# Two layers on a 128-node graph: scores placed behind attends, banks kept for them, splits and first mixes moved, last division in halves

## The chip, the core and the metric

The kernel runs on one core of one Trainium2 chip. The metric is the device time of one execution in microseconds. Engines are named as in the profile: PE is TensorE, DVE VectorE, ACT ScalarE, POOL GpSimd, SP SyncE, which here issues every DMA.

## The reference

The input is x, 128 batches of 128 nodes with 512 features, and one 128 by 128 adjacency matrix. Two layers follow each other:

```python
# layer 0
h = relu(layernorm(x))
x = x + (einsum('nm,bmd->bnd', adj, h) @ weight + bias)
# layer 1: masked attention, 8 heads of 64
h = relu(layernorm(x))
q, k, v = split(h @ w_qkv)
attn = softmax(where(adj == 0, -inf, q @ k.T * 64**-0.5))
o = (attn @ v) @ w_proj + b_proj
x = x + o + (layernorm(o) * gamma + beta)
```

All is float32. Where precision asks for it, the kernel splits both factors of a product into a high and a low part and adds three products in a faster number format (fp32r) instead of one plain float32 product.

## The kernel before

**Stages.** The first stage (`phase1`) does layer 0 batch by batch. For each batch it makes the statistics, the ReLU, the product with the adjacency matrix ("mix", L483), splits that product in three parts (L430 to L432), multiplies them with the split weight `wA` (L442, twelve matmuls of 512 columns for a batch), and adds (L450, L455). The first `FIRST` = 4 batches use a plain float32 product instead (L492), because the split weight isn't made yet; there a copy of the mix by ACT (L487) stands between mix and product. The results go to DRAM.

The second stage (`phase2_group`) does layer 1 in 32 groups of four batches, each group as two pairs. `fetch` reads a pair back, normalises it, transposes it through DRAM, and splits it in three parts in the tile `hp`, which has room for three pairs. A group computes Q and K for all four batches (L580, 96 matmuls), and V for each batch (L442 on `wv`, 12 each, summed into a `v` tile at L615 and L616). For each pair, `scores_of` computes the scores (L637, in 64-row halves of the PE array), masks them (L645), takes the row maximum (L650), the exponentials (L657), the reciprocal (L661) and the division (L662, POOL), and sends them through DRAM to be transposed. A group later, `rest_of` lets them land, transposes 32 by 32 blocks (L678), multiplies with V ("attend", L696, in 64-column halves of the array), projects, and adds the last normalisation. The projection takes the split weight `wA1` (L442), or, for the last three pairs, the plain one (L714).

A pair's `rank` counts from the end: rank 0 is the last pair, rank 1 the one before it, ranks 3 and 2 the two pairs of the group before. The pair of rank 0 isn't sent through DRAM: PE flips its tiles (L684).

**What sets the order.** Nothing is ordered by hand. Every operation is put into a `Plan` with its engine, an estimated length, the tiles that it reads and writes, and either a due time or, on PE, a wished time (`at`). `schedule` then walks through a model of the core: whenever an engine is free, it takes, of the operations whose inputs are there, the one with the smallest priority whose tiles have a free place. The programs of the engines follow that order. Three details matter here:

- Tiles share places by name. `ps` are the eight PSUM banks `b0` to `b7`; a pair's scores take two banks for each batch, an attend two, each split product two. `f0` to `f3` hold the scores (`s`) and the transposed probabilities (`pT`) of phase 2. `qk` has eight places, so a group's Q and K can only be overwritten when the scores of the group before are done.
- An operation that finds no free place is passed over, and a later one may take the place that it waits for (L139 to L156).
- An operation in split-array mode has the mark `tiled`. The plan counts 0.15 us (`turn`) for a change of mode, and an operation that keeps the mode has its priority improved by 2 (`stay`).

The parameter `early`, where it is given, is the earliest planned time at which an operation may start.

**Lines that matter.** The wait of the landings is the argument `gate` of `rest_of`; it is set at L590 and again at L610:

```python
        if rests:
            rests.pop(0)(gate)
        gate = scores(0)
        ...
        if len(rests) > 1:
            rests.pop(0)(gate)
        scores(1)
```

Of the kernel before, what the change touches and what calls it, by code (L numbers as in the profile page):

```python
# [15 lines left out]
P = 128  # L16
# [40 lines left out]
class Plan:  # L57
# [44 lines left out]
    def schedule(self):  # L102
# [22 lines left out]
        while len(order) < len(self.ops):  # L125
# [6 lines left out]
            for e in self.ENGINES:  # L132
# [5 lines left out]
                stay = p["stay"] if e == "PE" else 0.0  # L138
                for item in sorted(avail[e], key=lambda i: (i[0] - (stay if self.ops[i[1]].tiled == tiled else 0.0), i[1])):  # L139
                    o, taken = self.ops[item[1]], []  # L140
                    for b in o.bufs:
# [10 lines left out]
                    for b in taken:  # L152
                        b.slots.places[b.name], b.name = 0.0, None
                        b.slots.next -= 1
                else:
                    continue  # L156
# [37 lines left out]
    "stretch": 1.5, "margin": 0.4, "crowd": 2.0,  # L194
# [4 lines left out]
def kernel(  # L199
# [36 lines left out]
    def named(prefix, *numbers):  # L236
# [14 lines left out]
        "wA": group(["wA"]), "ident": group(["t8"]), "ident2": group(named("t", 8, 14)), "raw2": group(named("t", 20, 24)),  # L251
# [79 lines left out]
    op("DVE", 1.4, mask_ops, r=[adj_sb], w=[adj_sb, some, maskb], due=30)  # L331


    def split_weights(w, c, col, raw, low, due, gap):
# [3 lines left out]
        op("ACT", 0.63, lambda: nc.scalar.activation(h(), raw.ap, AF.Copy, scale=CUT), r=[raw], w=[(w, (0, part))], due=due)  # L338
        op("DVE", 0.69, lambda: nc.vector.tensor_tensor(low.ap, raw.ap, h().bitcast(F32), op=ALU.subtract),
           r=[raw, (w, (0, part))], w=[low], due=due + gap)  # L340
        op("ACT", 0.62, lambda: nc.scalar.activation(l(), low.ap, AF.Copy, scale=K), r=[low], w=[(w, (1, part))], due=due + 2 * gap)
        op("DVE", 0.69, lambda: nc.vector.scalar_tensor_tensor(s(), low.ap, K, h().bitcast(F32), op0=ALU.mult, op1=ALU.subtract),
           r=[low, (w, (0, part))], w=[(w, (2, part))], due=due + 2 * gap)
# [22 lines left out]
    def stats(srcs, how, place, due=None, plain=False, junk=None, first=None):  # L366
# [8 lines left out]
        if how == "DVE":  # L375
            for n, src in enumerate(srcs):
                def bn(n=n, src=src):
                    nc.vector.bn_stats(t.ap[:, 6 * n:6 * n + 6], src.ap)  # L378
                    nc.vector.bn_aggr(t.ap[:, 12 + 2 * n:14 + 2 * n], t.ap[:, 6 * n:6 * n + 6])
                op("DVE", 0.87, bn, r=[src], w=[(t, n)], due=dues[0], what="bn")  # L380
# [85 lines left out]
    def phase1(batches):  # L466
# [4 lines left out]
        t, arg = stats([X[i] for i in batches], "DVE" if batches[0] < FIRST + 2 else "ACT", "st1", junk=[View(junk, lambda ap: ap)] * 2)  # L471
        for n, i in enumerate(batches):
# [11 lines left out]
            MIX[i] = op("PE", 0.9, mix, r=[h0, adjT], w=[p], at=ti - (1 if i == 0 else 3.75), what="mix")  # L484
# [68 lines left out]
    rests, raw2, final = [], [], []  # L553

    def phase2_group(j):
# [54 lines left out]
        gate = scores(0)  # L610
        for n, i in enumerate(group):
# [3 lines left out]
            op("ACT", 0.6, lambda v=v, a=a: nc.scalar.activation(v.ap, a.ap, AF.Copy, scale=UP), r=[a], w=[v], due=tv + 2.5, what="vA")  # L615
            op("DVE", 0.69, lambda v=v, b=b: nc.vector.tensor_tensor(v.ap, b.ap, v.ap, op=ALU.add), r=[b], w=[v], due=tv + 4, what="vB")  # L616
# [3 lines left out]
        if not left:  # L620
# [3 lines left out]
            op("POOL", 0.6, lambda: make_identity(nc, ident2.ap), w=[ident2], what="ident", after=[b.writers[-1][1]])  # L624

    def scores_of(pair, place, QK, rank, at_scores):

        S = []
        for n, i in enumerate(pair):
# [8 lines left out]
            last = op("PE", 0.85, scores, r=list(QK.values()), w=ps, at=ts, what="scores", tiled=True)  # L638
# [19 lines left out]
            for g in range(4):  # L658
                op("ACT", 1.16, lambda g=g, exps=exps: exps((2 * g, 2 * g + 1)), r=[(mx, "m")], w=[(s, ("e", g)), (mx, g)],
                   due=ts + 6 + 2.3 * g + 9.2 * n if rank else ts + 4 + 1.2 * g + 4 * n, what="exp")  # L660
            op("DVE", 0.18, lambda mx=mx: nc.vector.reciprocal(mx.ap[:, H:], mx.ap[:, H:]), w=[mx], what="rec", due=ts + 15 + 9.2 * n)  # L661
            op("POOL", 1.93, lambda heads=heads, mx=mx: nc.gpsimd.tensor_tensor(  # L662
                heads().rearrange("p h q r -> p q h r"), heads().rearrange("p h q r -> p q h r"),
# [128 lines left out]
```

## Time and profile before

| | us |
|---|---|
| three runs: lowest, median, highest | 2163.84, 2164.19, 2164.22 |
| the profiled execution | 2163.97 |
| its span, first to last instruction | 2162.2 |
| PE busy | 2147.0 |
| DVE busy | 1721.4 |
| POOL busy | 1524.2 |
| ACT busy | 1480.0 |
| mean granted PE clock | 0.999 of full speed |

The span is what the trace shows; the execution's own time has 1.8 us more around it. PE is busy for 99% of the span, but ends of matmuls are modelled, so that a busy PE isn't PE at its peak: the spacing between the starts of matmuls tells more. In rows of a timeline or of the chain of waits, the first number is the start in us from the beginning of the span, the second the length; xN counts the instructions that the row merges; a bracket gives the idle time before the row and what ended it. A float32 matmul appears as two instructions.

### The profile page before, as it was taken

How to read it: one execution, taken by the hardware profiler on the slowest of the kernel's cores; microseconds unless marked ns; L12 is line 12 of the kernel's file. 1: busy time of each engine (PE TensorE's matmuls, PEld its weight loads, DVE VectorE, ACT ScalarE, POOL GpSimd, SP SyncE). 2: the span in 40 equal slices, each digit the busy share in tenths (PEclk: the TensorE clock that was granted, in tenths of full speed). 3: DMA queues.
4: the chain of work that ended last, by engine and by line, in shares of the span. 5: the costliest groups of instructions: out<-in, count | busy, mean ns of one | idle time of the engine just before them, and what ended most of it. 6: DMA issues, size and time to landing. Idle time of an engine off the chain costs nothing.

```text
span 2162.2 us, 40584 instructions
## 1 busy us (share of the span) xinstructions
PE 2147.0 (99%) x12811; PEld 1778.6 (82%) x12811; DVE 1721.4 (80%) x3271; ACT 1480.0 (68%) x4238; POOL 1524.2 (70%) x1276
## 2 busy tenths in 40 slices
PE   9999999999999999999999999999999999999998
PEld 7888888888878888888888888888888888888885
DVE  7998888885877778777777777878777777777777
ACT  7887777767666666666666666666666666666653
POOL 6887878784667666666667777777667777777755
PEclk9999999999999999999999999999999999999999
DMA  7766666665656666666655556566666666556653
GB/s 245 244 217 228 218 217 217 225 225 161 176 166 195 183 188 182 190 185 182 180 176 176 176 176 183 179 185 184 193 184 185 186 180 196 177 180 182 185 176 118
DMA packets 297863, 410.69 MB, mean 190 GB/s; under 512 B 33072, under 2 KB 163248, under 8 KB 297648
## 3 DMA queue, kind: packets, MB, share of 16 engines
q1 hardware_dynamic: 297648, 408.09, 62.0%
q8 instruction: 102, 1.67, 0.3%
q14 instruction: 113, 0.93, 0.1%
HBM read 207.68 MB, written 200.28 MB: 189 GB/s over the span
## 4 chain that ended last, share of the span: by engine, by line
PE 92%; DVE 1%; POOL 0%; DMA 0%; issue 0%; ACT 0%; SPq 0%; POOLq 0%; DVEq 0%; ACTq 0%
PE b L442 44%; PE b L580 32%; PE b L637 6%; PE b L696 5%; PE b L483 4%; DVE t L730 0%; POOL f L662 0%; DMA f<-d 0%; DVE t L728 0%; DMA out_dram<-t 0%; POOL m L384 0%; DVE m L378 0%; DVE t L716 0%; ACT t L539 0%; SPq L267 0%
## 5 line engine op out<-in xcount | busy, mean ns | idle before, releaser
L442 PE MATMUL b<-wA,t 128*128 128x512 f32 x2952 | 750.4, 393 | 2.2 <-DVE t L431 1.2
L580 PE MATMUL b<-hp,wqk 128*128 128x512 f32 x3072 | 738.8, 390 | 0.8 <-ACT t L587 0.8
L580 PEld LDWEIGHTS b<-hp,wqk 128*128 128x128 f32 x3072 | 574.1, 188 | 124.9 <-issue 4.5
L442 PEld LDWEIGHTS b<-wA,t 128*128 128x128 f32 x2952 | 544.7, 188 | 111.3 <-DVE t L431 2.0
L722 POOL TENSOR_TENSOR t<-t,t 128x512 f32<-128x512 f32 x126 | 163.3, 1297 | 419.9 <-DVE t L453 297.5
L657 ACT ACTIVATE f<-f,n 128x128 f32<-128x128 f32 x1024 | 397.0, 391 | 2.1
L442 PE MATMUL b<-wv,hp 128*128 128x512 f32 x1536 | 388.2, 395 | 0.8 <-DVE t L453 0.8
L442 PEld LDWEIGHTS b<-wv,hp 128*128 128x128 f32 x1536 | 283.2, 188 | 65.9 <-DVE t L453 1.2
L587 ACT ACTIVATE t<-b 128x512 f32<-128x512 f32 x256 | 151.7, 593 | 241.6 <-PE b L580 241.4
L645 DVE TENSOR_TENSOR f<-b,maskb 128x512 f32<-128x512 f32 x256 | 166.3, 683 | 138.0 <-PE b L696 74.2
L662 POOL TENSOR_TENSOR f<-f,n 128x1024 f32<-128x1024 f32 x128 | 246.1, 1923 | 31.1 <-DVE n L661 31.1
L430 ACT ACTIVATE t<-b 128x512 fp32r<-128x512 f32 x246 | 145.2, 590 | 106.4 <-PE b L483 83.4
L547 POOL TENSOR_TENSOR hp<-t,hp 128x512 fp32r<-128x512 f32 x128 | 163.5, 1300 | 55.1 <-ACT hp L546 55.1
L588 DVE TENSOR_TENSOR t<-b,t 128x512 f32<-128x512 f32 x256 | 172.8, 676 | 34.8 <-PE b L580 24.3
L657 ACT ACTIVATION_READ_ACCUMULATOR f<-f,n 128x1 f32 x1024 | 194.5, 190 | 0.0
L431 DVE TENSOR_TENSOR t<-b,t 128x512 fp32r<-128x512 f32 x246 | 167.0, 679 | 22.5 <-ACT t L430 22.1
L432 DVE SCALAR_TENSOR_TENSOR t<-t,b 128x512 fp32r<-128x512 f32 x246 | 166.5, 677 | 0.0
L726 POOL TENSOR_TENSOR t<-t,t 128x512 f32<-128x512 f32 x122 | 158.0, 1295 | 9.5
L550 POOL TENSOR_TENSOR hp<-hp 128x512 fp32r<-128x512 f32 x128 | 164.0, 1303 | 0.6
L725 POOL TENSOR_TENSOR t<-t,gamma_b 128x512 f32<-128x512 f32 x122 | 158.0, 1295 | 8.1 <-ACT t L724 8.1
L678 DVE STREAM_TRANSPOSE f<-f 128x1024 f32<-128x1024 f32 x126 | 156.0, 1238 | 5.8 <-DMA f<-d 5.0
L650 DVE TENSOR_REDUCE n<-f 128x8 f32<-128x1024 f32 x128 | 155.1, 1212 | 1.3
(119 smaller groups left out, 3133.5 us busy)
## 6 DMA issues: line engine op xcount, KB each, us to landing
d<-f SPq DMA_DIRECT2D x126, 512.0 KB, 3.3
f<-d SPq DMA_DIRECT2D x504, 128.0 KB, 4.4
t<-x1d SPq DMA_DIRECT2D x128, 256.0 KB, 4.2
d<-t SPq DMA_DIRECT2D x128, 256.0 KB, 3.0
t<-d SPq DMA_DIRECT2D x512, 64.0 KB, 3.7
t<-x1b SPq DMA_DIRECT2D x128, 256.0 KB, 3.8
out_dram<-t SPq DMA_DIRECT2D x128, 256.0 KB, 3.4
t<-in_x_dram SPq DMA_DIRECT2D x91, 256.0 KB, 3.0
```

Source lines behind the costliest of these rows:

```text
L431: op("DVE", 0.69, lambda: nc.vector.tensor_tensor(l.ap, p.ap, h.ap.bitcast(F32), op=ALU.subtract), r=[p, h], w=[l], what=name + "l")
L432: op("DVE", 0.69, lambda: nc.vector.scalar_tensor_tensor(s.ap, h.ap.bitcast(F32), UP, p.ap, op0=ALU.mult, op1=ALU.subtract), r=[p, h], w=[ ...
L442: nc.tensor.matmul(p.ap, lhsT=parts[m][2]()[:, c], rhs=w.ap[:, m, c, :], start=start and c == 0, stop=stop and c == C - 1)
L547: op("POOL", 1.35, lambda ht=ht, h=h, l=l: nc.gpsimd.tensor_tensor(l(), ht(), h().bitcast(F32), op=ALU.subtract), r=[h1, HP[i, 0]], w=[HP[ ...
L550: op("POOL", 1.38, lambda l=l, s=s: nc.gpsimd.tensor_tensor(s(), s().bitcast(F32), l().bitcast(F32), op=ALU.subtract), r=[HP[i, 1]], w=[HP ...
L580: nc.tensor.matmul(p.ap, lhsT=wqk.ap[:, which, c, col:col + P], rhs=hp[:, pick, :, which, c, :], start=start and c == 0, stop=stop and c = ...
L588: op("DVE", 0.69, lambda r=r, b=b: nc.vector.tensor_tensor(r.ap, b.ap, r.ap, op=ALU.add), r=[b], w=[r], due=tg + (4 if g < 7 else 2), what ...
L645: op("DVE", 0.68, lambda e=e, heads=heads, ps=ps: nc.vector.tensor_tensor(heads()[:, e * C:(e + 1) * C], ps[e].ap.rearrange("p c (q r) -> ...
L657: nc.scalar.activation(v[:, h], v[:, h], AF.Exp, bias=mx.ap[:, h:h + 1], scale=scale, accum_out=mx.ap[:, H + h:H + h + 1])
L662: op("POOL", 1.93, lambda heads=heads, mx=mx: nc.gpsimd.tensor_tensor(heads().rearrange("p h q r -> p q h r"), heads().rearrange("p h q r ...
L722: op(eng, us, lambda x1=x1, o=o, unit=unit: unit.tensor_tensor(x1.ap, x1.ap, o.ap, op=ALU.add), r=[o], w=[x1], due=tl + (3 if rank > 1 els ...
L725: op("POOL", 1.32, lambda o=o: nc.gpsimd.tensor_tensor(o.ap, o.ap, gamma_b.ap, op=ALU.mult), r=[gamma_b], w=[o], due=tl + 7, what="gamma")
```

## The change

The edits fall into five groups.

- **Planner.** An operation in split mode that finds no free place now keeps its kind of place: for the rest of that pass, no lower operation that needs a new place of that kind is taken. If the array is already in split mode and enough places come free within 0.6 us (`wait`), PE takes nothing until then.
- **Order in phase 2.** Scores of ranks above 2 must follow the last attend that was put into the plan. The landings of the second pair are gated by the fifth product of Q and K, no longer by the first scores of the group. Block transposes are due 3 us earlier, the two halves of V's sum 1.5 and 2 us.
- **Start.** The mask may not start before 13.5, the statistics of batch 1 not before 6.2, the splits of the first weight not before 12 to 16.5; mixes of batches 0 to 5 are wished 4.9 us ahead of their product, not 3.75. (Batch 0 wished 1 ahead, as before.)
- **Weight splits.** The twelve splits of `w_qkv`, each with its load, go with every third pair of phase 1 from the seventh pair on, not with every pair from the fifth on.
- **End.** Rank 2 projects with the split weight; the exponentials, reciprocal and division of rank 1 have earlier due times; rank 0 takes reciprocal and division in two halves of four heads, each flip waiting for its half; the identity for the flips is made in the tile of the means, near the end of the last group's due times.

```diff
@@ schedule
                 stay = p["stay"] if e == "PE" else 0.0
+                held = []
                 for item in sorted(avail[e], ...):
                     o, taken = self.ops[item[1]], []
+                    if held and any(b.slots in held for b in o.bufs if b.slots and not b.name):
+                        continue
...
                     for b in taken:
                         b.slots.places[b.name], b.name = 0.0, None
                         b.slots.next -= 1
+                    if o.tiled:
+                        held.append(b.slots)
+                        if tiled:
+                            soon = sorted(v for v in (b.slots.places[n] for n in b.slots.names) if v is not None)
+                            want = sum(x.slots is b.slots and not x.name for x in o.bufs)
+                            if len(soon) >= want and soon[want - 1] <= t + p["wait"]:
+                                held = None
+                                break
                 else:
+                    held = None
+                if held is None:
                     continue
...
-    "stretch": 1.5, "margin": 0.4, "crowd": 2.0,
+    "stretch": 1.5, "margin": 0.4, "crowd": 2.0, "wait": 0.6,
@@ start
-    op("DVE", 1.4, mask_ops, r=[adj_sb], w=[adj_sb, some, maskb], due=30)
+    op("DVE", 1.4, mask_ops, r=[adj_sb], w=[adj_sb, some, maskb], due=30, early=13.5)
...
+                       early=6.2 if batches == [1] else 0.0)
...
-            MIX[i] = op("PE", 0.9, mix, r=[h0, adjT], w=[p], at=ti - (1 if i == 0 else 3.75), what="mix")
+            MIX[i] = op("PE", 0.9, mix, r=[h0, adjT], w=[p], at=ti - (1 if i == 0 else 4.9 if i < FIRST + 2 else 3.75), what="mix")
...
-        split_weights(wA0, c, 0, raw0[c], buf("raw", [P, D]), time1(FIRST) - 7 + 1.5 * c, 0.5)
+        split_weights(wA0, c, 0, raw0[c], buf("raw", [P, D]), time1(FIRST) - 7 + 1.5 * c, 0.5, 12.0 + 1.5 * c)
...
-        k = j - FIRST // 2 - 2
-        if 0 <= k < 12:
+        k, odd = divmod(j - FIRST // 2 - 4, 3)
+        if 0 <= k < 12 and not odd:
@@ phase2_group
-        gate = scores(0)
+        scores(0)
...
-            op("ACT", 0.6, ... w=[v], due=tv + 2.5, what="vA")
-            op("DVE", 0.69, ... w=[v], due=tv + 4, what="vB")
+            op("ACT", 0.6, ... w=[v], due=tv + 1, what="vA")
+            op("DVE", 0.69, ... w=[v], due=tv + 2, what="vB")
...
-            op("POOL", 0.6, lambda: make_identity(nc, ident2.ap), w=[ident2], what="ident", after=[b.writers[-1][1]])
+            op("POOL", 0.6, lambda: make_identity(nc, ident2.ap), w=[ident2], what="ident", due=t0 + 40)
@@ scores_of
-            last = op("PE", 0.85, scores, r=list(QK.values()), w=ps, at=ts, what="scores", tiled=True)
+            last = op("PE", 0.85, scores, r=list(QK.values()), w=ps, at=ts, what="scores", tiled=True,
+                      after=attends[-1:] if rank > 2 else [])
...
-                   due=ts + 6 + 2.3 * g + 9.2 * n if rank else ts + 4 + 1.2 * g + 4 * n, what="exp")
+                   due=ts + 6 + 2.3 * g + 9.2 * n if rank > 1 else ts + 4 + 1.2 * g + 4 * n, what="exp")
...
+            else:
+                for e in range(2):
+                    some = slice(e * C, (e + 1) * C)
+                    op("DVE", 0.16, ... nc.vector.reciprocal(mx.ap[:, H + e * C:H + (e + 1) * C], ...), what="rec", ...)
+                    op("POOL", 1.0, ... nc.gpsimd.tensor_tensor(heads()[:, some] ..., op=ALU.mult), what="div", ...)
@@ rest_of
-                op("DVE", 1.24, lambda pT=pT: nc.vector.transpose(pT.ap, pT.ap), w=[pT], what="pT", due=at_attend[n] - (6 - 3 * n))
+                op("DVE", 1.24, lambda pT=pT: nc.vector.transpose(pT.ap, pT.ap), w=[pT], what="pT", due=at_attend[n] - (9 - 3 * n))
...
-                    op("PE", 0.6, flip, r=[s, ident2], w=[flips[e]], at=at_attend[n] - 3 + e, what="flip")
+                    op("PE", 0.6, flip, r=[(s, ("e", 2 * e)), (s, ("e", 2 * e + 1)), ident2], w=[flips[e]], at=at_attend[n] - 3 + e, what="flip")
...
+        attends.append(att)
...
-            if rank > 2:
+            if rank > 1:
                 parts = split_left(PO[n], "op")
...
-    ident2 = buf("ident2", [P, P])
+    ident2 = means
```

## The prediction, made before the changed kernel ran

> **What bounds the kernel now.** I read the page first, then the chain of waits, TensorE's waits, the chain inside one period of the second layer, and last the timeline around each place the edits touch. Page, busy time by engine, and the chain's summary:
>
> ```profile
> PE 2147.0 (99%) x12811; PEld 1778.6 (82%) x12811; DVE 1721.4 (80%) x3271; ACT 1480.0 (68%) x4238; POOL 1524.2 (70%) x1276
> ...
> PE 92%; DVE 1%; POOL 0%; DMA 0%; issue 0%; ACT 0%; SPq 0%; POOLq 0%; DVEq 0%; ACTq 0%
> ```
>
> TensorE sets the time. What can be won is what TensorE spends beyond its own matmuls: mode changes, a few stalls, start and end. Chain of waits, one period (start, us, what):
>
> ```profile
> 1264.62 6.35 PE b L580 x28
> 1270.96 1.90 PE b L696 x32
> 1272.86 1.99 PE b L637 x32
> 1274.85 14.74 PE b L442 x64
> 1289.58 1.99 PE b L637 x32
> 1291.57 2.04 PE b L442 x8
> 1293.61 3.63 PE b L580 x16
> 1297.23 1.90 PE b L696 x32
> 1299.13 2.04 PE b L580 x8
> ```
>
> L696 is attend, L637 scores, both in the split array. A 512-column matmul takes 3.63/16 = 0.227 us, yet eight of them after a split block take 2.04, not 1.81. A block and what it delays: joint 1270.96 to 1289.58 less 64 x 0.227 = 4.1; scores alone 1289.58 to 1293.61 less 1.81 = 2.2; attend alone 2.1. So joining two lone blocks saves about 0.2 us (from the starts of single matmuls 0.20; these rows give 0.23; I take 0.2). Over the run, TensorE's timeline has 30 joint blocks, 34 lone scores, 32 lone attends. Periods like this one have no stall at all.
>
> TensorE's waits, and its timeline at the start, at 120 us and at the end (start, length, idle before):
>
> ```profile
> 8.85 2.38 PE L483 MATMUL b<-t,t 128*128 128x128 f32 x16 [0.59 <-ACT t L475]
> ...
> 20.65 7.13 PE L492 MATMUL b<-f,t 128*128 128x512 f32 x16 [0.68 <-ACT t L487]
> ...
> 30.18 1.20 PE L442 MATMUL b<-wA,t 128*128 128x512 f32 x4 [0.61 <-ACT t L430]
> ...
> 117.36 5.37 PE L442 MATMUL b<-wA,t 128*128 128x512 f32 x20
> ...
> 127.52 1.19 PE L442 MATMUL b<-wA,t 128*128 128x512 f32 x4 [1.17 <-DVE t L431]
> ...
> 2118.61 2.14 PE L442 MATMUL b<-wv,hp 128*128 128x512 f32 x8 [0.79 <-DVE t L453]
> ...
> 2126.34 7.03 PE L714 MATMUL b<-t,t 128*128 128x512 f32 x16
> ...
> 2145.74 3.70 PE L714 MATMUL b<-t,t 128*128 128x512 f32 x8 [0.69 <-ACT t L710]
> ...
> 2151.15 3.70 PE L714 MATMUL b<-t,t 128*128 128x512 f32 x8 [0.69 <-ACT t L710]
> ```
>
> And two DVE rows that explain the lone blocks:
>
> ```profile
> 1298.31 0.69 DVE L645 TENSOR_TENSOR f<-b,maskb 128x512 f32<-128x512 f32 x1 [2.40 <-PE b L696]
> ...
> 1341.97 1.24 DVE L678 STREAM_TRANSPOSE f<-f 128x1024 f32<-128x1024 f32 x1
> ```
>
> The lone scores at 1289.5 put their sums into four PSUM banks; their masking runs only at 1298.3, after the lone attend has freed an `f` tile. So early scores gain nothing downstream and block half of PSUM for 9 us.
>
> **The Trainium skill.** "TensorEngine Tiling (Array Packing)", Key Properties, says that changing the tiling mode drains TensorE; the trace agrees, 0.23 us after each block, and joining saves only part of two changes. "PSUM — Partial Sum Buffer", Terms, gives eight banks per partition: four for one pair's scores and two for an attend are six, so the joint block nearly fills PSUM; the trace shows the first joint block of each period doing so without a stall. "SBUF — State Buffer", the section on the two separate sides, says that VectorE and GpSimd lock a shared port for whole instructions; agreed, the masking-weight subtraction L339 took 1.68 us instead of 0.68 at 123.4 beside a GpSimd add. This matters for what GpSimd work is moved.
>
> **The change part by part.**
>
> *Scores after attend, banks held.* Of 34 lone scores, two in the first group have no attend to wait for, and ranks 2 and 0 are not bound: 30 remain, 30 x 0.2 = 6.0 us. Is the attend there in time? Lone scores ran at 1341.48; the second transposed probability tile was made at 1341.97 to 1343.2, due 3 us before the attend; its last landing was issued by 1334.2 (1332.69 for 1.50 us) and lands a median 4.4 us later, 1338.6. With the due time 3 us earlier and the landings (eight of 128 KB per pair on SP's queue) no longer gated by the first scores of the group but by the group's fifth QK product, the transpose can end by about 1340, so the attend is ready at the old place of the scores. Behind the waiting scores stand the next group's QK matmuls, which overwrite the QK tiles; V of the next group (2 x 12 x 0.227 = 5.4 us) can fill. Scores' own softmax is not delayed: its masking waits for the attend today. Holding banks and the allowed 0.6 us pause inside split mode add a TensorE stall of 0 to 0.6 us per block where banks free late; no row of before shows it. I take 0, because the 4-bank hold disappears and the existing joint block has none, and keep the upper end for the range. V sums due 1.5 to 2 us earlier only free banks sooner.
>
> *Start.* The six mask operations (DVE, 5.02 to 6.41) and the first bn of batch 1 stand ahead of batch 0's shift at 7.34; its GpSimd power had ended at 5.73. Moved past 13.5 (and 6.2), the shift comes at about 5.9, ReLU ends near 6.9, and the first mix starts when the warming matmuls end, 8.2 instead of 8.85. The w0 splits (2 ACT, 2 DVE, four times, about 0.65 us each) leave the same stretch; they must be done by 27 us, and 5.5 us of DVE then stand between 12 and 27, where the w_qkv splits of 23 to 30 us make room. With the mixes 1.15 us ahead in priority, mixes 2 to 5 run before the plain product they used to follow, and the two copies waited for (0.84 and 0.78 us by starts) are covered. TensorE then has six mixes of 8 x 0.111 and four plain products of 8 x 0.429 from 8.2: 8.2 + 5.3 + 13.7 = 27.2, some 0.2 for hand-overs, 27.4 against 30.18. Taken 2.7; between 1 (ReLUs late, X landings) and 3.
>
> *w_qkv splits spread.* Twelve times one 256 KB load on SP's queue, 2 ACT, 2 DVE, from every pair of images to every third pair, the last at about 294 us, needed at 475. DVE was busy 38.35 of 40 us in 80 to 120, 32.47 in 300 to 340 without splits. The stalls near 120 (5.37 for 20 matmuls that take 4.8 elsewhere, and 1.17) are this DVE crowding: 0.57 + 1.17 = 1.75 us gone. After it DVE has 32.5 + 40/21.8 x 2 x 0.69 = 35 of 40: covered. If not, 0.
>
> *End.* Rank 2's projection by split parts: per image 12 x 0.227 = 2.72 for 8 x 0.429 = 3.43, two images, 1.4 us less. It adds three DVE operations net per image (about 2 us), hidden while TensorE still has 25 us of work. An attend with banks held runs when ready (its transposes ended 2114.2, it ran 2121.59), which brings the last masking (2123.61, waiting for it) forward; earlier exponentials, reciprocals and a division in two halves (L662 1.92 us becomes two of about 1.0, bound 0.9 to 1.4, on GpSimd; reciprocal 0.16 twice) let the last flips and attends go before rank 1's second product. Then one of the two waits for the copy (0.9 us by starts each) is filled and the 0.95 before 2118.61 may go; I count 0.9 + half of 0.95. Identity on GpSimd, moved from the end into `means` (two small operations, 0.5 us), leaves SP's queue at 2126.3. End: 1.4 + 0.9 + 0.5 = 2.8; between 0 and 4. The 7.4 us after the last matmul (2154.85 to 2162.2) stay.
>
> Single stalls at 459 (0.55) and 625 (1.0) I leave as they are.
>
> Sum: 6.0 + 2.7 + 1.75 + 2.8 = 13.25. The profiled execution took 2163.97 (span 2162.2 and 1.8 around it); 2163.97 - 13.25 = 2150.7. The median of the runs is 0.2 above that execution, so 2150.9, said as 2151.0.
>
> **Rivals.**
>
> *A. Joining is paid back by banks.* Attend and scores take six banks at once beside fillers; a pause of about 0.2 us in each of some 30 blocks eats the 6.0: 2157. For: eight banks only, DVE at 79% in a period must drain four score banks and two attend banks. Against: the existing joint block.
>
> *B. The edges give little.* Start and end are chains of small waits; another takes each place (DVE has 32.15 of the last 40 us): joins and spread splits alone, 7.75, with perhaps 1 us of edge: 2155.
>
> *C. The change doesn't join.* Attends stay late, scores leave the split mode for want of a bank: 2163.97 - 7.2, 2157 again.
>
> *D. Slower.* QK of the next group now stands behind scores, hence behind attend. If the second transpose ends later than 1341.5 + 5.4 = 1346.9, the V fillers are used up and TensorE idles each period for the rest. It ends at 1343.2 now: 3.7 us of slack. At 4.15 us later the loss is 0.44 x 30 = 13.25, all of the gain: from there it is slower; at 4.5 us later 0.8 x 30 - 13.25 is +11, 2175. For: tiles `f` are four, scores and transposes share them, landings now come earlier and could take the tiles in the wrong order. Against: the first pair works that way, and data land by 1338.6.
>
> **How the numbers follow.** Forecast 0.57 (own range 2147 to 2154), A and C together 0.19, B 0.13, D 0.11. A measurement of this kernel can hardly tell less than 0.2% (4.3 us) from no change, so faster means below 2159.9. D is mostly slower but partly within that band (0.03); A and C reach into it (0.06). Faster 0.83, same 0.09, slower 0.08. The range: low 2146, which is every listed stall removed (6.0 + 3 + 1.75 + 4 + 1.5 = 16.3, 2147.7) and some of the 0.23 of the rows; high 2160, which leaves out D and the worst of A.
>
> **What would show it.** Right: nearly every L696 block followed by L637, about 60 joint blocks, a period shorter by 0.2 us; the first L442 at about 27.4; no stall at 118 to 128; L714 x32 instead of x48 and at most one idle of 0.7 before it. Wrong: PE idle rows naming L645, L430 to L432 or L678 in every period (A, D); lone blocks as many as before (C); new idle before L492 or at the end (B).

## The result, and the profile after

The changed kernel takes 2160.26 us (median of 22 runs, 2156.90 to 2164.79); the kernel before took 2164.64 beside it (22 runs, 2163.66 to 2166.32). The ratio is 0.998, 95% interval 0.9973 to 0.9987: 4.4 us faster, where 13.25 were forecast, and 0.3 us above the upper end of the range. The profiled execution took 2160.06, its span 2158.3.

Engines' busy time, and the summary of the chain of waits, from the page of the changed kernel:

```profile
PE 2143.3 (99%) x12819; PEld 1782.2 (83%) x12819; DVE 1715.7 (79%) x3279; ACT 1496.3 (69%) x4238; POOL 1525.1 (71%) x1278
...
PE 90%; DVE 4%; DMA 3%; issue 1%; SPq 1%; ACT 0%; POOL 0%; POOLq 0%; DVEq 0%; ACTq 0%
```

PE is busy 3.7 us less and still bounds the kernel, but DVE and DMA together have gone from 1% of the chain to 7%: PE now waits for them, directly or through a bank, in places where it did not.

Where the time went is read from the starts of the same matmuls in both traces (the 576th Q and K matmul, and so on). The work up to each is nearly the same, so a difference between two rows of this table belongs, but for one reservation below, to the stretch between them. After less before, us, negative is earlier:

| up to | forecast | measured | of this stretch: forecast | measured |
|---|---|---|---|---|
| first matmul on the split weight | -2.7 | -2.75 | -2.7 | -2.75 |
| first Q and K product | -4.45 | -0.54 | -1.75 | +2.21 |
| Q and K of group 30 | -10.45 | -3.07 | -6.0 | -2.53 |
| last matmul | -13.25 | -5.03 | -2.8 | -1.96 |
| end of the span | -13.25 | -3.91 | 0 | +1.12 |

(The few joins after group 30 are counted in the third row of the forecast.) The reservation: in the changed order, Q and K of a group stand now before, now after some other products, in a cycle of four groups, and the distance to before swings with it. Group 30 is the most favourable place; groups 28, 29 and 31 stand at -1.81, -1.13 and -0.97. So up to 2 us of the third row may belong to the fourth; their sum, -4.49 of -8.8, doesn't depend on it, nor do comparisons of group 30 between kernels that share the order. Every stretch but the first fell short. In the changed kernel's line numbers split products are L455, mixes L497, Q and K L594, scores L651, attend L721, plain last products L740, flips L709; V's sum is L630, the block transposes L703 and L557.

PE's timeline of the changed kernel at the start, at 120 us, around one joint block, and at the end (start, length, idle before):

```profile
27.43 2.99 PE L455 MATMUL b<-wA,t 128*128 128x512 f32 x12
...
33.42 1.21 PE L455 MATMUL b<-wA,t 128*128 128x512 f32 x4 [0.80 <-DVE t L444]
35.42 1.19 PE L455 MATMUL b<-wA,t 128*128 128x512 f32 x4 [0.79 <-DVE t L445]
...
38.72 4.22 PE L455 MATMUL b<-wA,t 128*128 128x512 f32 x16 [0.29 <-DVE t L444]
...
125.19 2.98 PE L455 MATMUL b<-wA,t 128*128 128x512 f32 x12
...
1235.27 1.97 PE L721 MATMUL b<-f,t 128*64 128x128 f32 x32
1237.16 1.38 PE L651 MATMUL b<-t,t 64*128 64x128 f32 x18
1238.75 1.16 PE L651 MATMUL b<-t,t 64*128 64x128 f32 x14 [0.21 <-DVE l L395]
...
2124.57 0.66 PE L709 MATMUL b<-means,f 128*128 128x128 f32 x4 [0.95 <-POOL f L687]
...
2142.68 7.13 PE L740 MATMUL b<-t,t 128*128 128x512 f32 x16
```

*Start.* The first split product begins at 27.43 (30.18 before), but four matmuls at 33.4 and four at 35.4 wait 0.8 us each for the split of their input. By the mix of batch 12 the changed kernel is 0.58 us behind: 3.3 us lost in 28 us. DVE's timeline names what stood there:

```profile
29.71 1.36 DVE L352 TENSOR_TENSOR t<-t,wqk 128x512 f32<-128x512 f32 x1
31.11 1.65 DVE L355 SCALAR_TENSOR_TENSOR wqk<-t,wqk 128x512 fp32r<-128x512 f32 x1
32.69 0.68 DVE L444 TENSOR_TENSOR t<-b,t 128x512 fp32r<-128x512 f32 x1
```

L352 and L355 are the first `w_qkv` split, which isn't needed before 475. It stands ahead of L444, whose result PE waits for, and both its steps take at least twice their usual 0.68 us, while GpSimd works at 29.24 to 32.2 (the sums L517, 1.29 us, and L491, 1.66). "SBUF — State Buffer" in the Trainium skill, the section on the two separate sides, says that a VectorE operation with two inputs in SBUF is locked out for the whole of a GpSimd instruction that reads SBUF. The trace agrees: L352 ends at 31.07 and L355 at 32.76, each 0.54 to 0.55 us after the GpSimd instruction that was running when it began. (The L339 that the prediction calls a masking-weight subtraction is this same operation in the kernel before, a step of a weight's split.)

*At 120 us* the stalls of 0.57 and 1.17 are gone, as forecast; twelve matmuls take 2.98 there.

*Joint blocks.* There are 54 instead of 30, with 10 lone scores and 10 lone attends left. In every fourth group one pair still does not join. But the scores block at 1237 is broken: 0.68 us more than its usual 1.79 from first to last start. The same holds at 821.6 (0.32), 1029.3 (0.50), 1652.6 (0.46) and 2108.9 (1.06), 3.0 us in all; before the change no scores block has such a gap. The chain of waits around the one at 1237 shows why:

```profile
1233.69 2.00 DMA t<-d
...
1235.82 0.06 DVE t L557
...
1236.45 0.65 DVE t L466
...
1238.14 0.56 DVE t L630
...
1238.77 1.14 PE b L651 x14
```

The second half of the scores needs a bank which V's sum L630 has still to read (the trace names no bank; the comparison below bears the reading out). The sum itself has long had its inputs (in experiment 9 it runs at 1230.92); it begins 2.8 us after the attend, because it stands on DVE behind a transpose (L557) that waits for a landing from DRAM, and behind what queued up after that. In all stalled blocks before 2100 L630 begins 2.4 us or more after the attend; where it begins 1.1 us after (1859.66) or 1.9 (1445.23), PE does not stop. (That holds for one place in the cycle of four groups. In other blocks, at 1425.6 and 1009.7, an L630 that begins 2.9 and 3.2 us after the attend stops nothing.)

Other traces confirm it. The change and experiments 1, 3, 4 and 6 run the same sequence of matmuls from the first Q and K product to group 30, so the seven joint blocks at this place of the cycle can be compared in five traces, 35 blocks. In the 24 in which L630 begins at most 1.91 us after the attend, the scores are whole. In the 11 in which it begins 2.24 to 3.45 us after, they are broken, by that delay less 2.11 us, to within 0.01 each time: 0.13 at a delay of 2.24, 0.68 at 2.79, 1.34 at 3.45. (Two more broken blocks, at another place of the cycle in experiments 1 and 3, follow the delay less 1.76.) DVE's waits for landings grew: L703 waits 31 times, 37.8 us, for the landed probabilities, 5 times and 5.0 us before.

*End.* The plain last products come as two runs of 16 with neither wait for the copy, one flip waits 0.95 us, and the last matmul starts 5.03 us earlier. Then 1.12 us are given back after it. DVE's timeline:

```profile
2149.86 0.69 DVE L742 TENSOR_TENSOR t<-b,bp_b 128x512 f32<-128x512 f32 x1 [0.62 <-PE b L740]
2150.47 0.74 DVE L754 SCALAR_TENSOR_TENSOR t<-t,m,gamma_b 128x512 f32<-128x512 f32 x1
2151.12 0.69 DVE L391 BATCH_NORM_STATS2 m<-t 128x6 f32<-128x512 f32 x1
```

L754 belongs to the batch before the last. The last two products now start 3.5 us apart, before 5.4, so the last batch's statistics (L391) and what follows stand behind the other's final steps. Experiments bear this out: from the start of the last matmul to the end of the span it is 9.05 us here and 9.85 in experiment 2 (3.5 us apart), but 7.92 and 8.26 in experiments 4 and 6 (5.4 apart) and 7.93 before.

### The profile page after: what moved, and what is told of

It is laid out like the page before. It is cut to its first block, busy times and chain, and to the rows that moved or that the text cites. A ratio compares the mean times of both kernels' runs of the same rounds, so it can differ in the third digit from the quotient of the medians.

```text
span 2158.3 us, 40838 instructions
## 1 busy us (share of the span) xinstructions
PE 2143.3 (99%) x12819; PEld 1782.2 (83%) x12819; DVE 1715.7 (79%) x3279; ACT 1496.3 (69%) x4238; POOL 1525.1 (71%) x1278
## 4 chain that ended last, share of the span: by engine, by line
PE 90%; DVE 4%; DMA 3%; issue 1%; SPq 1%; ACT 0%; POOL 0%; POOLq 0%; DVEq 0%; ACTq 0%
PE b L455 44%; PE b L594 31%; PE b L651 5%; PE b L721 5%; PE b L497 5%; DMA f<-d 2%; SPq L280 1%; DMA t<-in_x_dram 1%; PE b L740 0%; DMA t<-d 0%; DMA t<-x1b 0%; DVE f L660 0%; DVE t L444 0%; DVE t L630 0%; DVE t L352 0%
## 5 line engine op out<-in xcount | busy, mean ns | idle before, releaser
L455 PE MATMUL b<-wA,t 128*128 128x512 f32 x2976 | 744.8, 394 | 2.6 <-DVE t L445 1.5
L594 PE MATMUL b<-hp,wqk 128*128 128x512 f32 x3072 | 721.1, 390 | 0.2 <-DVE f L660 0.2
L594 PEld LDWEIGHTS b<-hp,wqk 128*128 128x128 f32 x3072 | 575.4, 188 | 122.9 <-POOL l L397 2.5
L455 PEld LDWEIGHTS b<-wA,t 128*128 128x128 f32 x2976 | 547.8, 188 | 114.7 <-DVE t L445 2.8
L455 PE MATMUL b<-wv,hp 128*128 128x512 f32 x1536 | 381.6, 393 | 0.0
L748 POOL TENSOR_TENSOR t<-t,t 128x512 f32<-128x512 f32 x126 | 163.5, 1297 | 283.2 <-DVE t L466 232.4
L455 PEld LDWEIGHTS b<-wv,hp 128*128 128x128 f32 x1536 | 284.5, 188 | 63.1 <-issue 0.2
L678 POOL TENSOR_TENSOR f<-f,n 128x1024 f32<-128x1024 f32 x126 | 241.4, 1922 | 45.2 <-DVE n L677 42.7
L444 DVE TENSOR_TENSOR t<-b,t 128x512 fp32r<-128x512 f32 x248 | 169.1, 682 | 22.7 <-ACT t L443 20.9
L703 DVE STREAM_TRANSPOSE f<-f 128x1024 f32<-128x1024 f32 x126 | 155.2, 1232 | 38.2 <-DMA f<-d 37.8
L560 ACT ACTIVATE hp<-t 128x512 fp32r<-128x512 f32 x128 | 79.8, 631 | 112.9 <-DVE t L557 96.9
```

What stands on the lines that cost most here:

```text
L444: op("DVE", 0.69, lambda: nc.vector.tensor_tensor(l.ap, p.ap, h.ap.bitcast(F32), op=ALU.subtract), r=[p, h], w=[l], what=name + "l")
L455: nc.tensor.matmul(p.ap, lhsT=parts[m][2]()[:, c], rhs=w.ap[:, m, c, :], start=start and c == 0, stop=stop and c == C - 1)
L594: nc.tensor.matmul(p.ap, lhsT=wqk.ap[:, which, c, col:col + P], rhs=hp[:, pick, :, which, c, :], start=start and c == 0, stop=stop and c = ...
L748: op(eng, us, lambda x1=x1, o=o, unit=unit: unit.tensor_tensor(x1.ap, x1.ap, o.ap, op=ALU.add), r=[o], w=[x1], due=tl + (3 if rank > 1 els ...
```

## The experiments

The differences are against the changed kernel where nothing else is said; ratios are against the kernel before, run beside each. That kernel took 2164.64 beside the change, but 2164.04 beside experiments 1 to 4, 2164.18 beside 5 to 8 and 2163.97 beside 9 and 10. Differences from the change are therefore uncertain by about 0.5 to 0.7 us from this alone; where it matters, a second figure is given, worked out against the kernel before in each case. Times up to a place are of the one profiled execution, which can lie 2 us from the median.

**1. The `w_qkv` splits not before their due time.** Does the first split cost the 3.3 us?

```diff
-            split_weights(..., raw, raw, time1(2 * j), 2.0)
+            split_weights(..., raw, raw, time1(2 * j), 2.0, time1(2 * j) - 6)
```

> The changed kernel with one edit more: a w_qkv split may not be planned before 6 us ahead of its batch's time, so the first two no longer stand among the first products. My theory: the first product starts at 27.4 us as now, and the 3.3 us that TensorE loses between 30 and 42 us, waiting for L444 and L445 behind two w_qkv splits on VectorE, come back: about 2157.0 us, some 7.5 below the kernel before; the mix of batch 12 near 52.2 us and not 55.5. Rival (the start is bound by the general load of VectorE, or by landings of x): another wait takes the place, less than 1 us comes back, 2159.5 or more.

Measured 2157.45 (2153.70 to 2158.38), ratio 0.9967 (0.9954 to 0.9979), 2.8 us better than the change (2.2 by the kernels before), as expected. The first split's subtraction L352 now runs at 54.8. PE's timeline where the stalls were:

```profile
27.63 3.00 PE L455 MATMUL b<-wA,t 128*128 128x512 f32 x12
...
31.28 3.01 PE L455 MATMUL b<-wA,t 128*128 128x512 f32 x12
...
34.93 3.89 PE L455 MATMUL b<-wA,t 128*128 128x512 f32 x16
```

No wait is left, and the mix of batch 12 stands 2.38 us ahead of before, the first Q and K product 4.48: the sum of the two terms of the forecast for this stretch (2.7 and 1.75) comes out to 0.03 us. Of these about 3.9 us more than in the change, 3.2 remain at the end of the span; the scores blocks still stall (3.8 us in four blocks).

**2. Joining undone**: no keeping of places, no pause, no order after the attend, old due times of V's sums and transposes, old gate.

```diff
-                held = []
...
-                      after=attends[-1:] if rank > 2 else [])
...
-        scores(0)
+        gate = scores(0)
...
```

> The changed kernel without what joins the blocks: no held banks and no pause, scores not after attends, gate and due times of phase 2 as before; start and end as changed. My theory: 24 joins of 0.2 us are worth 4.8, but stalls inside joint blocks (0.2 to 1.1 us each, 2 to 3 us in all) and new waits take more than half of it back, so undoing costs 1.5 to 3 us against the changed kernel: 2162 to 2163 us, and no stall inside a scores block. Rival (the joins bring all of their 4.8, and the loss is only at start and end): 2165 us. Second rival (the joins bring nothing or harm): 2160 us or less.

Measured 2167.67 (2165.44 to 2171.27), ratio 1.0017 (1.001 to 1.0024), slower than before and outside of all three expectations. Against before it stands at -0.76 us at the first Q and K product and at exactly -0.76 in group 30: without joining the second layer neither gains nor loses. The loss is all at the end, 4.4 us, where PE waits for the half division (L673 here, flip L695):

```profile
2129.60 0.66 PE L695 MATMUL b<-means,f 128*128 128x128 f32 x4 [2.97 <-POOL f L673]
```

The edits of the end presuppose the others: rank 0's masking waits for the attend before it (L707, done at 2122.8, as in the kernel before), so the flips, now placed ahead of the last products, wait instead of filling. So this run does not price joining alone. That masking shows in DVE's timeline:

```profile
2122.83 1.29 DVE L646 TENSOR_TENSOR f<-b,maskb 128x512 f32<-128x512 f32 x2 [1.03 <-PE b L707]
```

**3. The start undone**: mask, statistics, first weight's splits, mixes and the spread of `w_qkv` as before.

```diff
-    op("DVE", 1.4, mask_ops, ..., due=30, early=13.5)
+    op("DVE", 1.4, mask_ops, ..., due=30)
...
-        k, odd = divmod(j - FIRST // 2 - 4, 3)
-        if 0 <= k < 12 and not odd:
+        k = j - FIRST // 2 - 2
+        if 0 <= k < 12:
```

> The changed kernel with the start as before: mask, statistics of batch 1, w0 splits and mixes at their old times, and the w_qkv splits at every pair from the fifth. My theory: the start is a wash: 2.75 us won up to the first product and 1.6 us at 118 to 128, 3.3 us lost at 30 to 42 and 0.6 later, net 0.5 at the first Q and K: 2160.8 us, first product at 30.2, stall of 1.2 us near 127 back. Rival (what is won at the start is kept to the end): 2163 us or more.

Measured 2159.61 (2157.93 to 2162.13), ratio 0.9981 (0.9974 to 0.9987). The first split product is back at 30.86 and the stall at 127 too (1.18 idle, 1.17 before the change), and the first Q and K product comes 1.80 us later than in the change and 5.74 later than in experiment 1; still the median is 0.65 us under the change's, and as far under the kernel before (4.4 us) as the change. (This profiled execution, 2161.63, is 2 us slower than its median.) So the edits of the start with the spread bring nothing in the change that the medians can show. In the traces they are worth 5.7 us at the first Q and K product when the first split keeps out of the way, and that split takes 3.9 of them back.

**4. The end undone**: rank 2 on the plain weight, old due times for rank 1; halves of rank 0 kept.

```diff
-            if rank > 1:
+            if rank > 2:
...
-                   due=ts + 6 + 2.3 * g + 9.2 * n if rank > 1 else ts + 4 + 1.2 * g + 4 * n, what="exp")
+                   due=ts + 6 + 2.3 * g + 9.2 * n if rank else ts + 4 + 1.2 * g + 4 * n, what="exp")
...
```

> The changed kernel with rank 2 projected by the plain weight again and the due times of rank 1 as before; the halves of rank 0 stay. My theory: the split projection is worth its 1.4 us of TensorE time and the earlier due times little: 2161.5 us, L740 x48 or the like. Rival (VectorE bounds the end, so the two or three operations more for each batch of rank 2 cost what TensorE wins): 2160 us, no difference.

Measured 2161.02 (2158.60 to 2164.55), ratio 0.9986 (0.9979 to 0.9993): 0.8 us worse (1.4 by the kernels before), with a spread too wide to fix it closely. Its profiled execution is the lucky kind: the second layer has the change's order of matmuls, yet from the first Q and K product to group 30 it gained 4.3 us where the change gained 2.5, with a single broken scores block before group 30. The order alone does not decide how many blocks break; it differs from run to run, with the start of V's sums. (That the landings of the run move these is likely from the waits shown, not shown by an experiment.) From group 30 to the end it loses 0.9 us where the change gains 0.8.

**5. Places not kept**: only the planner's edit undone.

```diff
-                held = []
...
-                    if held and any(b.slots in held for b in o.bufs if b.slots and not b.name):
-                        continue
...
```

> The changed kernel without the planner's edit (no held banks, no pause); scores still after attends, all else as changed. In its order 44 pairs have attend and both scores together, 14 have one of the two scores apart, 17 lone single scores. My theory: holding banks only keeps the second scores in the block; without it some 14 to 17 changes of mode of 0.3 us come back (4 to 5 us), but the second scores no longer stall inside a block (1 to 2 us): 2162.5 to 2164 us. Rival (the pause itself is the cost): 2159 us or less.

Measured 2164.65 (2163.83 to 2166.60), ratio 1.0003 (0.9995 to 1.0011): without the places kept, nothing of the change's 4.4 us is left. (That is no share of its own: each experiment undoes its edits beside all the others, and the losses don't add up.) It was expected to cost a little less. Holding and pausing were undone together; their parts are not shown. PE's timeline shows the way it is lost (L708 is attend, L638 scores):

```profile
1444.95 1.97 PE L708 MATMUL b<-f,t 128*64 128x128 f32 x32
1446.85 1.16 PE L638 MATMUL b<-t,t 64*128 64x128 f32 x16
1447.94 1.20 PE L442 MATMUL b<-wv,hp 128*128 128x512 f32 x4
1449.07 1.16 PE L638 MATMUL b<-t,t 64*128 64x128 f32 x16
```

The attend is followed by the scores of one batch only; for the second batch the plan has no place free, four matmuls of V take PE, and the other batch's scores come later, a lone block with mode changes of its own. There are 59 joint blocks here, more than in the change, but 15 of them have the scores of one batch only, and 21 scores blocks are lone. The order after the attend brings the two together; only the places kept hold a pair's scores together.

**6. The last division whole.**

```diff
-            if rank:
...
-            else:
-                for e in range(2):
...
-                    op("PE", 0.6, flip, r=[(s, ("e", 2 * e)), (s, ("e", 2 * e + 1)), ident2], ...)
+                    op("PE", 0.6, flip, r=[s, ident2], ...)
```

> The changed kernel with the last division whole again (one reciprocal and one division of 1.92 us for each batch of rank 0, flips waiting for all of it). My theory: in the changed kernel the halves let the flips start early but they stall on the second half (1.0 us at 2123.3, the half division standing behind a 1.3 us addition on GpSimd), and the two last products then run back to back, so that VectorE's end is 1.1 us longer; undone, the end is at most 1 us slower: 2160.5 to 2161.5 us. Rival (the halves are what wins at the end): 2163 us.

Measured 2162.41 (2159.74 to 2163.13), ratio 0.9989 (0.9981 to 0.9998), 2.15 us worse than the change (2.6 by the kernels before); the rival's number was nearer. PE's timeline near its end (flip L699, division L677, copy L726):

```profile
2124.05 0.66 PE L699 MATMUL b<-means,f 128*128 128x128 f32 x4 [2.27 <-POOL f L677]
...
2143.85 3.70 PE L730 MATMUL b<-t,t 128*128 128x512 f32 x8 [0.69 <-ACT t L726]
2149.26 3.70 PE L730 MATMUL b<-t,t 128*128 128x512 f32 x8 [0.68 <-ACT t L726]
```

The flip waits 2.27 us instead of 0.95, and both waits for the copy are back. From group 30 to the end this trace loses 2.9 us where the change gains 0.8. So at the end of the kernel the halves pay most: 3.7 us there, against 1.8 for the edits of experiment 4.

**7. Experiment 1, and the first pair of a group fetched 4 us earlier.** If late landings ahead of V's sum break the scores, earlier ones should not.

```diff
-            fetch(group[2 * p:2 * p + 2], t0 - (37, 8)[p])
+            fetch(group[2 * p:2 * p + 2], t0 - (41, 8)[p])
```

> The kernel with the w_qkv splits held back (first experiment), and the first pair of each group fetched 4 us earlier in the plan; its order has 61 joint blocks and 5 lone ones instead of 54 and 20. My theory: seven joins more bring 1.4 us; but the planner still counts on a landing earlier than the chip's, so the stalls inside the scores, behind block transposes of h1 that wait for their landing, stay (some of 0.3 to 0.9 us): 2155 to 2157 us. Rival (joins are worth what they were forecast and the stalls are chance): 2154 us.

Measured 2151.07 (2150.42 to 2151.59), ratio 0.9940 (0.9927 to 0.9952), 4 us better than expected; the rival's 2154 was nearer. The chain of waits around the same place as above:

```profile
1229.74 1.90 PE b L721 x32
1231.63 1.99 PE b L651 x32
1233.62 1.13 PE b L455 x4
```

Now 61 blocks are joint, with 3 lone scores and 3 lone attends, and no scores block is broken between 475 and 2090. From group 10 to group 30 the kernel gains 0.22 us in every group on before. The waits of the transposes for the probabilities fell to 4.4 us (6 times). Those of L557 did not fall: 20.3 us, 29 times, and they break nothing in this order.

**8. The same, with the planner told that the normalised rows land 1.6 us later than it assumes.** Are those 20.3 us worth anything?

```diff
-                    o.end = pipe + p["landing"]
+                    o.end = pipe + p["landing"] + (1.6 if o.what == "h1 in" else 0.0)
```

> As the kernel fetched early, and the planner counts 1.6 us more until the transposed h1 has landed, so that no block transpose of h1 is placed before its data. 61 joint blocks, 5 lone. My theory: the waits of VectorE for that landing (14.9 us in all, 20 times, in the changed kernel) fall below 5 us, no scores block stalls by more than 0.1 us, and the spread of the runs shrinks to that of the kernel before: 2153.5 to 2155 us. Rival (the stalls come from banks, not from the landing): scores still stall, 2156 us or more.

Measured 2150.74 (2149.58 to 2151.49), ratio 0.9938 (0.9925 to 0.9952). L557 waits once, 0.3 us, and the time is the same within the spread, below both expectations. So in this order the waits for landings cost nothing in themselves; what counts is what stands behind them on DVE.

**9. V's sum first.** The changed kernel; only in the finished order of DVE each second sum of V is moved up, past transposes and statistics, to where its inputs are there.

```diff
+        for o in [o for o in order if o.what == "vB"]:
+            i, mine = order.index(o), {b.name for b in o.bufs if b.slots}
+            while order[i - 1].start > o.ready and order[i - 1] not in o.preds and not mine & {...}:
+                order[i], order[i - 1] = order[i - 1], o
+                i -= 1
```

> The changed kernel, its order kept but for one thing: each second half of a V sum (L630) is moved up in the finished order to where its inputs are ready, ahead of block transposes, statistics and sums that stood before it on VectorE; 54 joint blocks as before. In the changed kernel the second scores stalled only in blocks in which that V sum began 2.4 us or more after the attend, behind block transposes that waited for a landing; where it began within 1.9 us nothing stalled. My theory (that sum holds the bank that the scores wait for): between 550 and 2050 us no scores block is longer than 2.0 us, and the steady groups win 0.1 to 0.15 us each against the kernel before; 2157.5 to 2159 us. Rival (the bank is one of the projection's, or the transposes themselves are late): stalls in scores remain, 2160 us or more.

Measured 2157.87 (7 runs, 2157.14 to 2159.55), ratio 0.9971 (0.996 to 0.9982): 2.4 us better than the change (1.7 by the kernels before), as expected. The runs span 2.4 us, not 7.9, though they are 7 and not 22. The profiled execution is the slowest of them, 2159.55, with a start 1.1 us worse than the change's. The block at 1237 in DVE's timeline, then in PE's (V's sum L635, scores L656):

```profile
1230.92 0.69 DVE L635 TENSOR_TENSOR t<-b,t 128x512 f32<-128x512 f32 x1 [0.60 <-PE b L460]
```

```profile
1235.27 1.97 PE L726 MATMUL b<-f,t 128*64 128x128 f32 x32
1237.17 2.06 PE L656 MATMUL b<-t,t 64*128 64x128 f32 x32
```

The sum runs 7 us earlier than in the change, and the scores go through. No scores block of the second layer before 2100 is broken. The trace alone would not prove it, for experiments 4 and 6 have one broken block each there without this edit; with the median and the delays above it does. From group 10 to group 30 the gain is 0.09 us a group, a little less than expected. It is also less than in experiments 4 and 6 (0.13 and 0.14), for this trace has more waits between other matmuls there, 7.47 us against 6.9 and 6.6.

**10. Experiment 8, with the last batch's final steps 8 us ahead in priority.** What does the tail cost?

```diff
-            tl = at_proj[n] + 5
+            tl = at_proj[n] + 5 - (8 if rank == 0 and n else 0)
```

> As the kernel fetched early with the longer landing, and the last batch's operations have due times 8 us earlier, so that its statistics no longer stand behind the batch before it on VectorE. My theory: with the two last products back to back, VectorE takes turns between two batches, 1.1 us of the end; with the last batch first, about half of it comes back, as VectorE then has the other batch's two operations to do instead: last matmul to end 8.3 to 8.7 us instead of about 9.1, 2150.3 us. Rival (VectorE has the same work in any order): no difference, 2150.7.

Measured 2150.03 (2149.58 to 2151.08), ratio 0.9937 (0.9924 to 0.9949). From the start of the last matmul to the end of the span it is 8.82 us, against 9.06 in experiment 8, 9.05 in the change and 7.93 before: a fifth of the loss returns, where half was expected. (The medians, 0.7 us apart over five runs each, don't settle it.) The statistics now come first, but the final steps of both batches still stand together at the end. This version has the lowest median, 14 us under the kernel before and 10 under the change.

## Why the prediction was wrong in size

The direction was right and the size three times too large. Its own steps, one by one:

- **Start, 2.7.** Right up to the first split product (2.75), in part by luck: the first mix began at 7.41 and not at 8.2, because the warming matmuls took 3.70 us and not 4.38, and a wait of 0.75 before the second mix, which the forecast lacked, took that back. What failed after it is the sentence that "the `w_qkv` splits of 23 to 30 us make room". They were to be later; the diff delays only their due times and gives them no earliest time. An operation that is ready is taken whenever its engine has nothing better, so the first split moved from 23.8 to 29.7, just ahead of the first batches' own splits, and cost 3.3 us. The last of the twelve ran at about 177 us, not at 294. Experiment 1 takes the first away (there the last runs at 289) and gets the sum of both terms of this stretch.
- **Spread splits, 1.75.** The stalls at 118 to 128 are gone, as forecast, though the splits were spread only half as far as it assumed. A smaller one, 0.32 idle, appears at 134.
- **Joins, 30 times 0.2.** The price was right and the number wrong: 24. (The rows shown give 0.24, not 0.23, and of lone attends there were 33 and the last pair's in two halves, not 32; the sum doesn't change by it.) Between the Q and K of groups 10 and 30 all traces have the same 6400 full and small matmuls, so what exceeds even spacing can be counted by kind of place (us over 20 groups):

| | before | after | V's sum first | experiment 8 |
|---|---|---|---|---|
| joint blocks of 40 | 20 | 35 | 35 | 40 |
| into, between and out of blocks | 17.18 | 15.84 | 15.85 | 15.34 |
| other places between full matmuls | 8.01 | 6.90 | 7.47 | 5.44 |
| inside scores blocks | 0.03 | 1.69 | 0.03 | 0.04 |
| start of group 10 to start of group 30 | 1039.33 | 1038.55 | 1037.47 | 1034.93 |

Twenty joins give 4.40 in experiment 8, 0.22 each. Fifteen should have given 3.3 in the change; the scores blocks took 1.7 of it, small waits between the other matmuls 0.8 (most at the 13th and 14th matmul after a block; their cause is open), and 0.8 was left.
- **"I take 0" for the pause of the banks.** This is the step that failed in the second layer. I reasoned that "the existing joint block has none". In the joint blocks of before no V sum begins later than 0.7 us after the attend; in the new ones some do, because a bank's last reader is a DVE operation in a queue with waits for landings. Rival A had the mechanism, eight banks and their draining by DVE, at an assumed 0.2 us in 30 blocks; it is 0.3 to 1.1 us in five, of which the last has another cause (below). Experiment 9 removes the four by the order of DVE alone; in experiments 7 and 8, with an earlier fetch and so another order, they don't occur.
- **The stall at 625**, taken to stay, is gone (1.0 us); the one at 459 stayed (0.55).
- **End, 2.8.** Both waits for the copy went, the last matmul gained 2.0 from group 30 on, with a stall of 1.06 in the last group's scores; in experiment 8 the same stretch gives 2.82 (both with the reservation on group 30). The halves carry most of it (experiment 6). That "the 7.4 us after the last matmul stay" was wrong: 1.1 more, because the last two batches now end closer together.

Rival A (6.0 lost) and rival B (4 lost) came in together in part, 2151 + 10 = 2161, and no case had both. That is where the chances were wrong: they were treated as excluding each other, though one edit's failure says nothing on the other's. C and D did not occur: the blocks do join, and no period waits for Q and K behind the scores.

That experiments 7, 8 and 10 end at 2151.07, 2150.74 and 2150.03 shows that the time forecast, 2151.0, was there to be had; but with two edits that the change does not contain, and with 61 joins instead of 54, so this does not make the forecast right.

Open: how to mend the scores block of the last groups, near 2100 to 2109, that is broken in all these joined versions. V's sum is not the cause there: experiment 9 moved it ahead, to 2104.78, and the break stays at 1.03. Its chain of waits names the masking of the block's own first scores (2109.29, 0.68 us long), after which the other scores follow at 2110.02. Open too: why in every fourth group one pair did not join until the fetch came earlier (readiness of its transpose is the likely cause, not shown); the flip's 0.95 us for the half division behind L748 on GpSimd, which no run removed.

## To carry to other kernels

When an edit makes operations of one engine stand together, ask for each resource that they need who reads it last, and what can stand ahead of that reader in its own queue; a reader that is ready, behind a transpose that waits for a landing, is late. A later due time only lowers a priority: to keep work out of a stretch it needs an earliest time. And price the end with what follows the last matmul: here two pieces that end together cost 1.1 us more after it than two that end in turn.

## What was not expected of the hardware

- Runs of the changed kernel differ more from each other than those of the kernel before: 2156.9 to 2164.8 against 2163.7 to 2166.3, 22 runs each. With V's sums moved ahead it is 2157.1 to 2159.6 (7 runs), with earlier fetches (experiment 7) 2150.4 to 2151.6 (5 runs), which points to landings; but fewer runs show less of a spread, and without the joins (experiment 2) it is 2165.4 to 2171.3 (18 runs), so the cause is not shown.
- Beside GpSimd, a small DVE operation loses more in proportion: the mask's first step took 1.29 us at 19.65 and ended at 20.94, just after GpSimd's sum L491 at 20.86 (0.23 before, at 5.02, with GpSimd all but idle), and one 128x512 split operation took 1.65 instead of 0.68.
- Joining two blocks is worth little at the change itself (0.092 going in, 0.145 coming out, less 0.148 between the two kinds: 0.09); the rest of the 0.22 us shows in the matmuls that follow a block.
